# Two-layer interaction network: the leftover products of layer 1 in batches of eight tiles instead of four

## The chip, the cores and the metric

The kernel runs on one core of a Trainium2 chip. A time is that of one execution on the device in microseconds; the kernel before took 2046.02 us (median of 5 runs, 2044.9 to 2047.05). The core's engines run side by side and meet through semaphores: TensorE (PE) multiplies matrices and writes PSUM, VectorE (DVE) does elementwise and reducing work, ScalarE (ACT) evicts PSUM, GpSimd (POOL) adds tiles in layer 2, SyncE (SP) issues most of the loads. ACT issues the stores.

## The reference

A batch of 4096 rows, each with 32 fields of 16 values, goes through two layers:

```python
def _cin_layer(out, x, W, b, gamma, beta):
    r, _, e = x.shape
    h = jnp.einsum('rne,rfe->rnfe', out, x).reshape(r, -1, e)
    h = jnp.einsum('rce,oc->roe', h, W) + b[None, :, None]
    return _batchnorm(h, gamma, beta)
h1 = _cin_layer(x, x, W1, b1, g1, beta1)
out, direct1 = (h1[:, :64], h1[:, 64:])
direct2 = _cin_layer(out, x, W2, b2, g2, beta2)
agg = jnp.concatenate([direct1, direct2], axis=1)
return agg.sum(axis=-1)
```

Layer 1 multiplies every field with every field of the same row (32 x 32 products) and mixes the products into 128 channels. `_batchnorm` takes mean and variance of a channel over all rows and values, so the statistics of layer 1 must be complete before layer 2 can scale its input. Layer 2 takes the first 64 of those channels as `out`. All of it is float32.

## The kernel before, in words

A site is one value of one row: 65,536 sites in 128 tiles of T = 512. A tile's result in layer 1 is one PSUM bank: 128 channels by 512 sites.

The product of field i and field j is that of j and i, so W1 is folded beforehand and layer 1 needs about half of the products. They fall into two parts:

- The main products: for each tile, DVE writes z, four blocks of 128 products (L387, `multiply_main`), and PE multiplies them with four blocks of weights (L428), into the tile's bank. A float32 matmul is two passes on PE, so a tile has eight.
- The leftovers: 16 products of fields 16 apart. They fill only 16 rows. Eight tiles (a GROUP) share one operand `r` of 128 partitions, 32 partitions to each of four tiles; two tiles t and t+4 share the same 32. DVE multiplies the two halves of r into `zr` once for eight tiles (L373). PE multiplies 32 rows of it for each of four tiles, side by side in the array, into the banks of those four tiles (L380, `add_leftovers`). The weights for the other tile's 16 rows are zero; `w1_sb[rows, 4]` belongs to the first four tiles of the eight and `w1_sb[rows, 5]` to the last four.

The loop at L400 to L455 runs over 124 tiles. At every fourth tile it takes four banks from the pool `psum` (six buffers; `factors` has the other two banks), lets PE do the leftovers of the four tiles first (they begin the sums), then the main products of one tile after another. For tiles 0 to 3 the leftovers come after the main products of tile 1: they end the sums of tiles 0 and 1 and begin those of 2 and 3 (FIRST = 2).

`finish(t)` (L337) evicts a bank: ACT writes e (for the statistics), kept (the 64 rows that layer 2 reads; stored to DRAM as `h` after every second tile) and ed (the other 64); DVE adds e to the statistics (L115) and, after every second tile, sums ed over the embedding (L364, `sum_direct`). It is called for tile t-1 once tile t's matmuls are written. There are two buffers of e, four of z, four of the operands a and b of the main products, one each of r and zr.

The last four tiles (ENDING, L458 to L546) are done in halves of 64 channels: first the kept halves of all four, with whose statistics layer 2 can begin, then the direct halves. Their leftovers (L461, `add_leftovers_halves`) use the zr of the same group of eight as tiles 120 to 123.

The loads are on SP's queue in program order: a and b of a tile (L294, 512 KB each), `load_rem` for r (L279, 512 KB), and, spread over the loop (EARLY), the differences `xs` and the first operands of layer 2. The order of instructions on an engine is fixed when the program is built: a scheduler places them by their readiness in its own view of the program, `tc.issue_after` puts one behind another, and `queue` keeps a chain of them in order.

Of the kernel before, what the change touches and what calls it, by code (L numbers as in the profile page):

```python
# [38 lines left out]
FP = mybir.dt.float32  # L42
AF = mybir.ActivationFunctionType
ALU = mybir.AluOpType
AX = mybir.AxisListType

P = 128
# [3 lines left out]
T = 512  # L51
NC = HALF // T
NT = 2 * NC
# [4 lines left out]
GROUP = 8  # L58
# [6 lines left out]
FIRST = 2  # L65
# [5 lines left out]
def tile_cin(ctx: ExitStack, tc: tile.TileContext, xa, xb, xr, w1, w1m, w2, bn, out):  # L71
    nc = tc.nc
# [8 lines left out]
    psum = ctx.enter_context(tc.tile_pool(name="psum", bufs=6, space=bass.MemoryType.PSUM))  # L81
    factors = ctx.enter_context(tc.tile_pool(name="factors", bufs=2, space=bass.MemoryType.PSUM))
# [145 lines left out]
    def queue(engine, make):  # L228

        with tc.issue_after(lasts[engine].ins) if engine in lasts else nullcontext():  # L230
            lasts[engine] = make()
        return lasts[engine]
# [4 lines left out]
    begun = factors.tile([P, T], FP, tag="f", name="begun")  # L237
# [25 lines left out]
    with ExitStack() as one:  # L263
        lpool = one.enter_context(tc.tile_pool(name="lpool", bufs=4))
        rpool = one.enter_context(tc.tile_pool(name="rpool", bufs=1))
# [9 lines left out]
        def load_rem(g):  # L275

            r = rpool.tile([P, 2 * T], FP, tag="r", name="r")
            with tc.issue_after(loads[-1].ins) if loads else nullcontext():
                nc.sync.dma_start(r, bass.AP(xr.tensor, xr.offset + g * P * 2 * T, [[2 * T, P], [1, 2 * T]]))  # L279
            return r  # L280
# [25 lines left out]
        w1_sb = wpool.tile([P, 6, P], FP, tag="w1", name="w1_sb")  # L306
# [30 lines left out]
        pss = {}  # L337
# [4 lines left out]
        def finish(t):  # L342

            c, half = divmod(t, 2)
            ps = pss.pop(t)
            to = slice(half * KEEP, (half + 1) * KEEP)
            if half == 0:
                eds[c] = epool.tile([P, T], FP, tag="ed", name="ed")
                kept[c] = kpool.tile([KEEP, 2 * T], FP, tag="h", name="kept")
            ed = eds[c]  # L350
            e = opool.tile([P, T], FP, tag="e", name="e")
            nc.scalar.activation(e, ps, AF.Identity, bias=b1)  # L352
            stats1.add(e)
            h = kept[c]
            nc.scalar.activation(h[:, half * T : (half + 1) * T], ps[:KEEP, :], AF.Identity, bias=b1[:KEEP])
            if half == 1:
                nc.scalar.dma_start(hs[c], kept.pop(c))
            done = nc.scalar.activation(ed[to, :], ps[KEEP:, :], AF.Identity, bias=b1[KEEP:])  # L358
            if half == 1:
                sum_direct(c)  # L360
            return done

        def sum_direct(c):
            return nc.vector.tensor_reduce(  # L364
                d1[:, c * RT : (c + 1) * RT],
                eds.pop(c).rearrange("p (r e) -> p r e", e=EMB),
                AX.X,
                ALU.add,
            )

        def leftovers(r):
            zr = rpool.tile([P, T], FP, tag="zr", name="zr")
            nc.vector.tensor_tensor(zr, r[:, :T], r[:, T:], ALU.mult)  # L373
            return zr

        def add_leftovers(t, zr, begun=0):

            for k in range(4):
                rows = slice(32 * k, 32 * (k + 1))
                nc.tensor.matmul(  # L380
                    pss[t + k], w1_sb[rows, 4 + t % GROUP // 4, :], zr[rows, :], start=k >= begun, stop=k < begun
                )

        def multiply_main(z, a, b, k):

            n = k.stop - k.start
            return nc.vector.tensor_tensor(  # L387
                z[:, k],
                a.rearrange("p (a t) -> p a t", a=2)[:, k].unsqueeze(2).to_broadcast([P, n, 2, T]),
                b.rearrange("p (b t) -> p b t", b=2).unsqueeze(1).to_broadcast([P, n, 2, T]),  # L390
                ALU.mult,
            )

        def multiply_chunk(z, a, b, k, j):
            to = slice(k * T, (k + 1) * T), slice(j * T, (j + 1) * T)
            return nc.vector.tensor_tensor(z[:, k, j], a[:, to[0]], b[:, to[1]], ALU.mult)

        ending = NT - ENDING
        main = [load_main(t) for t in range(FIRST)]
        r = load_rem(0)  # L400
        for t in range(NT - ENDING):
            s = t % GROUP
            if s == 4 and t + 4 < NT:
                r = load_rem(t // GROUP + 1)
            if FIRST <= t + 1 < NT:
                main.append(load_main(t + 1))
            if s == 0 and t > 0:
                zr = leftovers(r)
            z = zpool.tile([P, 2, 2, T], FP, tag="z", name="z")
            if t < FIRST:  # L410
                for k in range(2):
                    for j in range(2):
                        product = multiply_chunk(z, *main[0], k, j)
            else:

                for k in (slice(0, 1), slice(1, 2)) if t == FIRST else (slice(0, 2),):
                    product = multiply_main(z, *main[0], k)
            main.pop(0)
            if t == FIRST - 1:
                with tc.issue_after(product.ins):  # L420
                    zr = leftovers(r)
            if s % 4 == 0:
                for k in range(4):
                    pss[t + k] = psum.tile([P, T], FP, tag="ps", name="ps")
            if s % 4 == 0 and t > 0:
                add_leftovers(t, zr)
            for m in range(4):
                nc.tensor.matmul(  # L428
                    pss[t],
                    w1_sb[:, m, :],  # L430
                    z[:, m // 2, m % 2, :],
                    start=t < FIRST and m == 0,
                    stop=t >= FIRST and m == 3,
                )
            if t == FIRST - 1:
                add_leftovers(0, zr, FIRST)
            if t > 0 and t < ending - 1:
                evicted = finish(t - 1)
            if t == 20:
                combine_weights()  # L440
                b1_swapped = const.tile([P, 1], FP, tag="b1s", name="b1_swapped")
                for x, y in ((low, high), (high, low)):
                    nc.scalar.activation(b1_swapped[x], b1[y], AF.Identity)
            if t == 0:
                continue
            with tc.issue_after(loads[-1].ins), tc.issue_after(product.ins), tc.issue_after(evicted.ins):
                if t == 12:
                    nc.vector.tensor_reduce(spread, select.rearrange("k i n f -> k (n f) i"), AX.X, ALU.max)
                if t == 14:
                    nc.vector.tensor_reduce(block, select.rearrange("k i n f -> k i (n f)"), AX.X, ALU.max)  # L450
                if t == 6:
                    nc.sync.dma_start(w2_sb, w2)
                for at, load in EARLY:
                    if t == at:
                        load()  # L455


        half_of = (low, high)  # L458

        def matmul(ps, w, z, start, stop):  # L460
            queue("pe", lambda: nc.tensor.matmul(ps, w, z, start=start, stop=stop))  # L461
# [13 lines left out]
        def add_leftovers_halves(banks, zr, direct, begun):  # L475

            for k in range(ENDING):
                rows = slice(32 * k, 32 * (k + 1))
                to = banks[k][half_of[(k + direct) % 2]]
                matmul(to, w1_sb[rows, 5, half_of[direct]], zr[rows, :], k not in begun, k in begun)  # L480

        zs = []
        for k in range(ENDING):
            if k + 1 < ENDING:
                main.append(load_main(ending + k + 1))
            zs.append(zpool.tile([P, 2, 2, T], FP, tag="z", name="z"))
            queue("dve", lambda: multiply_main(zs[k], *main.pop(0), slice(0, 2)))

        with tc.issue_after(lasts["dve"].ins):
            for t in (ending - 2, ending - 1):  # L490
                evicted = finish(t)
        banks = [psum.tile([P, T], FP, tag="ps", name="ps") for _ in range(ENDING)]
        add_leftovers_halves(banks, zr, 0, ())
        for c in range(NC - ENDING // 2, NC):
            ks = tuple(2 * c + half - ending for half in range(2))
            add_halves(banks, zs, 0, ks, True, True)
            h = kpool.tile([KEEP, 2 * T], FP, tag="h", name="kept")
            for half, k in enumerate(ks):
                at = half_of[half]
                to = h[:, half * T : (half + 1) * T]  # L500
# [28 lines left out]
        for c in range(NC - ENDING // 2, NC):  # L529
# [10 lines left out]
            for half, k in enumerate(ks):  # L540
                at = half_of[1 - half]
                bias = (b1, b1_swapped)[half][at]
                to = eds[c][half_of[half]]
# [6 lines left out]
    direct = const.tile([P, 2], FP, tag="direct", name="direct")  # L550
# [305 lines left out]
    for c in range(NC):  # L856
# [3 lines left out]
        for k, i in enumerate(STAGES):  # L860

            z = z2pool.tile([P, 4, 2, T], FP, tag="zz", name="zz")
            t = None
# [22 lines left out]
            if c > 0 or k > 0:  # L886
                t = sum_rest(z, b11, t2, (c, k) <= (1, 0), (c, k) == (NC - 1, 3))
# [121 lines left out]
```

## Time and profile before

| | |
|---|---|
| median of 5 runs | 2046.02 us (2044.9 to 2047.05) |
| profiled execution | 2045.4 us, span on the core 2043.7 us |
| layer 1 | 0 to about 490 us; layer 2 the rest |
| PE, DVE, ACT, POOL busy | 2027.5, 1959.4, 1185.4, 1487.3 us |
| leftovers in the main loop (L380) | 31 times four tiles, 248 passes |
| granted TensorE clock | 0.998 |

Layer 2, three quarters of the time, is not touched by the change. In layer 1 the matmuls of the tiles follow each other on PE; the other engines and the DMA prepare z ahead of it and clear the banks behind it. A row of the profile's groups or of its timeline has the line of the kernel, the engine, the operation and the tile that it writes and reads (out<-in). The profile counts a float32 matmul as two MATMUL instructions, one a pass.

### The profile page before, as it was taken

The page shows a single profiled execution, that of the slowest core. Times are in us where ns is not written, and L with a number is a line of the kernel's source. Part 1 is how long each engine was busy: PE and PEld are TensorE (multiplying, and loading weights), DVE is VectorE, ACT ScalarE, POOL GpSimd, SP SyncE. Part 2 cuts the span into 40 slices and gives each one's busy share as a digit, 9 for nine tenths or more (in the row PEclk, how much of TensorE's full clock was granted, in tenths as well). Part 3 has the DMA queues.
Part 4 walks back from the last instruction along what each step waited for, and adds up shares of the span by engine and source line. Part 5 has one row for each costly group of instructions (what it writes and reads, how often), then busy time and mean ns, then how long its engine had stood idle before and what let it go on. Part 6 is the DMA issues. An engine that isn't in the chain of part 4 may idle for free.

```text
span 2043.7 us, 24467 instructions
## 1 busy us (share of the span) xinstructions
PE 2027.5 (99%) x8500; PEld 888.5 (43%) x8500; DVE 1959.4 (96%) x1521; ACT 1185.4 (58%) x1914; POOL 1487.3 (73%) x525
## 2 busy tenths in 40 slices
PE   9999999999999999999999999999999999999997
PEld 3444444443344444444444444444444444444443
DVE  8998988998999999999999999999999999999998
ACT  4555555554566666655666556556656565566564
POOL 0000000002999999999999999999999999999996
PEclk9999999999999999999999999999999999999999
DMA  9999999996777777777776767777767777777661
GB/s 390 376 353 365 356 353 354 367 381 191 174 180 178 174 175 178 193 174 182 178 177 166 174 174 178 176 181 178 175 167 173 174 174 183 177 178 175 167 163 42
DMA packets 112380, 440.70 MB, mean 216 GB/s; under 512 B 13056, under 2 KB 13056, under 8 KB 103808
## 3 DMA queue, kind: packets, MB, share of 16 engines
q1 hardware_dynamic: 105840, 418.43, 73.1%
q10 hardware_dynamic: 6416, 20.72, 2.7%
q8 instruction: 66, 1.08, 0.2%
q14 instruction: 58, 0.48, 0.1%
HBM read 417.07 MB, written 22.02 MB: 215 GB/s over the span
## 4 chain that ended last, share of the span: by engine, by line
PE 98%; DVE 1%; issue 0%; POOL 0%; DMA 0%; ACT 0%; DVEq 0%; ACTq 0%; POOLq 0%
PE x L698 74%; PE ps L428 21%; PE ps L380 2%; PE ps L461 1%; DMA w1m_sb<-in_w1m 0%; POOL t L714 0%; DVE zz L667 0%; DVE d L934 0%; ACT u L659 0%; DVE both L662 0%; POOL t L703 0%; ACT both L659 0%; DVE d L833 0%; DVE t L662 0%; POOL w_sb L312 0%
## 5 line engine op out<-in xcount | busy, mean ns | idle before, releaser
L714 POOL TENSOR_TENSOR t<-zz,t 128x2048 f32<-128x2048 f32 (+1 forms) x260 | 1164.7, 4480 | 20.8 <-DVE t L662 1.0
L698 PE MATMUL x<-t,s_sb 128*64 128x512 f32 x2040 | 958.5, 592 | 0.4 <-POOL t L714 0.4
L698 PE MATMUL x<-zz,s_sb 128*64 128x512 f32 x2048 | 935.1, 593 | 0.0
L698 PE MATMUL x<-zz,w_sb 128*64 128x512 f32 x2056 | 760.7, 593 | 0.0
L703 POOL TENSOR_TENSOR t<-zz 128x512 f32<-128x512 f32 x255 | 327.1, 1283 | 515.6 <-DVE zz L667 515.2
L667 DVE TENSOR_TENSOR zz<-f,bx 128x2048 f32<-128x2048 f32 x255 | 582.7, 2285 | 19.6 <-ACT f L659 19.6
L659 ACT ACTIVATE f<-a,keep 128x512 f32<-128x512 f32 x512 | 398.2, 778 | 342.7 <-DVE zz L667 281.9
L667 DVE TENSOR_TENSOR zz<-f,b 128x2048 f32<-128x2048 f32 x255 | 583.0, 2286 | 0.1
L698 PEld LDWEIGHTS x<-t,s_sb 128*64 128x64 f32 x2040 | 279.3, 137 | 485.3 <-issue 457.0
L698 PE MATMUL x<-t,w_sb 128*64 128x512 f32 x1020 | 479.5, 593 | 0.0
L428 PE MATMUL ps<-z,w_sb 128*128 128x512 f32 x992 | 434.7, 596 | 1.7 <-POOL w_sb L312 1.6
L698 PEld LDWEIGHTS x<-zz,s_sb 128*64 128x64 f32 x2048 | 280.0, 137 | 246.4 <-issue 239.5
L387 DVE TENSOR_TENSOR z<-a,b 128x2048 f32<-128x2048 f32 (+1 forms) x127 | 288.2, 2271 | 42.6 <-PE ps L428 27.7
L428 PEld LDWEIGHTS ps<-z,w_sb 128*128 128x128 f32 x992 | 186.1, 190 | 248.9 <-issue 233.4
L698 PEld LDWEIGHTS x<-zz,w_sb 128*64 128x64 f32 x2056 | 239.7, 137 | 121.0 <-issue 119.0
L659 ACT ACTIVATE b<-zz 128x512 f32<-128x512 f32 x255 | 152.4, 598 | 187.2 <-DVE zz L667 187.2
L352 ACT ACTIVATE e<-ps,bn_sb 128x512 f32<-128x512 f32 x124 | 85.2, 687 | 218.0 <-PE ps L428 179.2
L662 DVE TENSOR_TENSOR t<-zz,b 128x512 f32<-128x512 f32 x255 | 174.0, 682 | 0.4
L698 PEld LDWEIGHTS x<-t,w_sb 128*64 128x64 f32 x1020 | 139.9, 137 | 0.0
L596 ACT ACTIVATE unread<-e,center 128x512 bf16<-128x512 f32 x122 | 86.2, 707 | 0.0
L358 ACT ACTIVATE ed<-ps,bn_sb 64x512 f32<-64x512 f32 x124 | 84.7, 683 | 2.3
L115 DVE BATCH_NORM_STATS2 stats<-e 128x6 f32<-128x512 f32 x124 | 84.9, 686 | 0.0
(103 smaller groups left out, 867.7 us busy)
## 6 DMA issues: line engine op xcount, KB each, us to landing
a<-h SPq DMA_DIRECT2D x256, 512.0 KB, 4.4
b<-in_xb SPq DMA_DIRECT2D x64, 1024.0 KB, 8.5
a<-in_xa SPq DMA_DIRECT2D x127, 512.0 KB, 7.1
b<-in_xb SPq DMA_DIRECT2D x127, 512.0 KB, 8.1
bx<-in_xb SPq DMA_DIRECT2D x64, 512.0 KB, 8.4
bx<-x SPq DMA_DIRECT2D x64, 512.0 KB, 10.1
h<-kept ACTq DMA_DIRECT2D x64, 256.0 KB, 5.7
r<-in_xr SPq DMA_DIRECT2D x16, 512.0 KB, 8.6
```

Of the source, the lines that this page charges most:

```text
L115: nc.vector.bn_stats(self.stats[:, self.at, :], h)
L352: nc.scalar.activation(e, ps, AF.Identity, bias=b1)
L358: done = nc.scalar.activation(ed[to, :], ps[KEEP:, :], AF.Identity, bias=b1[KEEP:])
L387: return nc.vector.tensor_tensor(z[:, k], a.rearrange("p (a t) -> p a t", a=2)[:, k].unsqueeze(2).to_broadcast([P, n, 2, T]), b.rearrange( ...
L428: nc.tensor.matmul(pss[t], w1_sb[:, m, :], z[:, m // 2, m % 2, :], start=t < FIRST and m == 0, stop=t >= FIRST and m == 3,)
L596: return nc.scalar.activation(unread, e[:, s], AF.Square, bias=center[:, s], accum_out=squares[:, s, c : c + 1])
L659: return queue("act", lambda: nc.scalar.activation(to, source, AF.Identity, **scale_bias))
L662: return dve(lambda: nc.vector.tensor_tensor(to, x, y, ALU.add))
L667: dve(lambda: nc.vector.tensor_tensor(z, a, b.rearrange("p (k q) t -> p k q t", k=2), ALU.mult))
L698: queue("pe", lambda: nc.tensor.matmul(self.of[x], w, b, start=start, stop=stop))
L703: queue("pool", lambda: nc.gpsimd.tensor_tensor(t2[:, 0], z[:, 1, 0], z[:, 0, 0], ALU.add))
L714: queue("pool", lambda: nc.gpsimd.tensor_tensor(t14[:, k, q], z[:, 2 + k.start : 2 + k.stop, q], twice[:, k, q], ALU.subtract))
```

## The change

The leftovers of eight tiles are done together. At every eighth tile t (8, 16, ..., 120) PE does the leftovers of tiles t-4 to t-1, which now end their sums, and those of t to t+3, which begin theirs. Tiles 4 to 7 of a group of eight begin with their main products. So up to eight banks are open at a time, and two of every eight tiles take theirs from `factors`. Nothing else is put between the two sets of four.

Eight tiles that share an r are now t-4 to t+3, so the host lays out xr in 17 groups instead of 16 (the first four and the last four tiles come twice), and the two blocks of leftover weights change places. `load_rem` is called for the next group at the second tile of each eight (for the second group at tile 3) instead of at the fifth. `finish` is called for tile t-4 instead of t-1, two tiles at a time at tiles 120 and 121. The last four tiles have a zr of their own, which DVE makes after the z of the first of them.

In the order of the built program, SP issues r ahead of the loads of tiles 4, 10, 18, 26, 34 and so on. Before, it stood ahead of tiles 5, 13, 21, 29. On DVE the next zr stands just after the statistics of the third of the four tiles that an episode of leftovers has ended.

```diff
+        def multiply_leftovers(zr, r):
+            return nc.vector.tensor_tensor(zr, r[:, :T], r[:, T:], ALU.mult)
+
         def leftovers(r):
             zr = rpool.tile([P, T], FP, tag="zr", name="zr")
-            nc.vector.tensor_tensor(zr, r[:, :T], r[:, T:], ALU.mult)
+            multiply_leftovers(zr, r)
             return zr
 
-        def add_leftovers(t, zr, begun=0):
+        def bank(t):
+            pool, tag = (psum, "ps") if t % GROUP < 6 else (factors, "f")
+            return pool.tile([P, T], FP, tag=tag, name="ps")
+
+        def ends_with_leftovers(t):
+            return t % GROUP >= 4 or t < FIRST
+
+        def add_leftovers(t, zr):
 
             for k in range(4):
                 rows = slice(32 * k, 32 * (k + 1))
-                nc.tensor.matmul(
-                    pss[t + k], w1_sb[rows, 4 + t % GROUP // 4, :], zr[rows, :], start=k >= begun, stop=k < begun
-                )
+                last = ends_with_leftovers(t + k)
+                w = w1_sb[rows, 4 + (t + 4) % GROUP // 4, :]
+                nc.tensor.matmul(pss[t + k], w, zr[rows, :], start=not last, stop=last)
...
-            if s == 4 and t + 4 < NT:
+            if s == 1 and t > 1 or t == 3:
+
                 r = load_rem(t // GROUP + 1)
...
             if s % 4 == 0:
                 for k in range(4):
-                    pss[t + k] = psum.tile([P, T], FP, tag="ps", name="ps")
-            if s % 4 == 0 and t > 0:
+                    pss[t + k] = bank(t + k)
+            if s == 0 and t > 0:
+                add_leftovers(t - 4, zr)
                 add_leftovers(t, zr)
             for m in range(4):
                 nc.tensor.matmul(
                     pss[t],
                     w1_sb[:, m, :],
                     z[:, m // 2, m % 2, :],
-                    start=t < FIRST and m == 0,
-                    stop=t >= FIRST and m == 3,
+                    start=ends_with_leftovers(t) and m == 0,
+                    stop=not ends_with_leftovers(t) and m == 3,
                 )
             if t == FIRST - 1:
-                add_leftovers(0, zr, FIRST)
-            if t > 0 and t < ending - 1:
-                evicted = finish(t - 1)
+                add_leftovers(0, zr)
+
+            if t >= ending - 2:
+                evicted = finish(t - 2)
+            elif t >= ending - 4:
+                for done in range(2 * t - ending, 2 * t - ending + 2):
+                    evicted = finish(done)
+            elif t >= 4:
+                evicted = finish(t - 4)
...
-            if t == 0:
+            if t < 4:
                 continue
...
-                matmul(to, w1_sb[rows, 5, half_of[direct]], zr[rows, :], k not in begun, k in begun)
+                matmul(to, w1_sb[rows, 4, half_of[direct]], zr[rows, :], k not in begun, k in begun)
...
             queue("dve", lambda: multiply_main(zs[k], *main.pop(0), slice(0, 2)))
+            if k == 0:
+                zr = rpool.tile([P, T], FP, tag="zr", name="zr")
+                queue("dve", lambda: multiply_leftovers(zr, r))
...
-    xr = np.stack([xt[:, :16], xt[:, 16:]], axis=2).reshape(NT // GROUP, GROUP // 4, 4, 16, 2, T)
-    xr = xr.transpose(0, 2, 1, 3, 4, 5).reshape(NT // GROUP, P, 2, T)
+
+    xr = np.stack([xt[:, :16], xt[:, 16:]], axis=2)
+    xr = np.concatenate([xr[:4], xr, xr[-4:]]).reshape(NT // GROUP + 1, GROUP // 4, 4, 16, 2, T)
+    xr = xr.transpose(0, 2, 1, 3, 4, 5).reshape(NT // GROUP + 1, P, 2, T)
```

## The prediction

> **What bounds the kernel now.** I read the page first: busy times, then the chain that ended last.
>
> ```profile
> PE 2027.5 (99%) x8500; PEld 888.5 (43%) x8500; DVE 1959.4 (96%) x1521; ACT 1185.4 (58%) x1914; POOL 1487.3 (73%) x525
> PE 98%; DVE 1%; issue 0%; POOL 0%; DMA 0%; ACT 0%; DVEq 0%; ACTq 0%; POOLq 0%
> ```
>
> TensorE (PE) is the bound in both layers; layer 1 is the first 490 us of 2043.7. What shortens PE's own work there shortens the kernel, as long as VectorE (DVE) and the DMA keep ahead. Next the timeline of PE in a settled stretch (start, length, engine, line):
>
> ```profile
> 99.39 1.14 PE L380 MATMUL ps<-zr,w_sb 32*128 32x512 f32 x8
> 100.46 14.00 PE L428 MATMUL ps<-z,w_sb 128*128 128x512 f32 x32
> 114.39 1.14 PE L380 MATMUL ps<-zr,w_sb 32*128 32x512 f32 x8
> ```
>
> Every four tiles take 15.00 us, to the hundredth: 32 instructions of the main products and eight of leftovers (four tiles side by side, two passes each). No stall. The same timeline cut so narrowly that single passes show, PE's weight loads (PEld) with it:
>
> ```profile
> 98.87 0.59 PE L428 MATMUL ps<-z,w_sb 128*128 128x512 f32 x1
> 99.39 0.31 PEld L380 LDWEIGHTS ps<-zr,w_sb 32*128 32x128 f32 x8 [0.76 <-issue]
> 99.39 0.71 PE L380 MATMUL ps<-zr,w_sb 32*128 32x512 f32 x4
> 99.92 0.61 PE L380 MATMUL ps<-zr,w_sb 32*128 32x512 f32 x4
> 100.46 0.70 PE L428 MATMUL ps<-z,w_sb 128*128 128x512 f32 x1
> 100.99 1.02 PE L428 MATMUL ps<-z,w_sb 128*128 128x512 f32 x2
> ```
>
> In the main stream a pass starts 0.43 us after the one before. Around the leftovers the four steps are 0.52, 0.53, 0.54 and 0.53. The first pass after each change of shape lasts 0.70 to 0.71 instead of 0.59 to 0.61, so it really begins 0.10 us into its row: the true steps are 0.62 (into the leftovers), 0.43 (between their two passes), 0.64 (back) and 0.43. So it is the two changes of shape that cost, about 0.2 us each, and not the passes between. Per episode: 15.00 - 34 x 0.4294 = 0.40 us.
>
> Last, who waits in DVE from 40 to 474 us, and the start of the run, where the cover is thinnest:
>
> ```profile
> DVE z L387 <- PE ps L428: 26.6, 39, 2.3
> DVE z L387 <- DMA b<-in_xb: 14.0, 11, 3.2
> ...
> 21.23 2.27 DVE L387 TENSOR_TENSOR z<-a,b 128x2048 f32<-128x2048 f32 x1
> 23.42 0.68 DVE L364 TENSOR_REDUCE d<-ed 128x32 f32<-128x512 f32 x1
> 24.38 1.14 PE L380 MATMUL ps<-zr,w_sb 32*128 32x512 f32 x8
> ...
> 17.41 0.69 ACT L352 ACTIVATE e<-ps,bn_sb 128x512 f32<-128x512 f32 x1 [8.40 <-PE ps L380]
> 19.39 0.69 ACT L352 ACTIVATE e<-ps,bn_sb 128x512 f32<-128x512 f32 x1
> ```
>
> DVE mostly waits for PE to free a z: it is four tiles ahead, a lead of 9 us (the z that ends at 121.49 is used at 130.46). ScalarE (ACT) evicts one tile every 1.98 us when it need not wait, beginning 1.16 us after the leftovers start (16.25).
>
> **The change, part by part.**
>
> *PE.* The main loop has the same 124 leftover matmuls, in 16 episodes instead of 31. If passes 2 to 3 follow like 1 to 2 (0.43), each of the 15 merges removes one pair of shape changes: 15 x 0.40 = **-6.0 us**. Bounds: nothing saved, if each four cost their 0.40 wherever they stand; no row offers more than 6.0. I take 6.0, since the step between passes 1 and 2 is the nearest row.
>
> [...] The row above shows eight loads, the second four for the same row groups, begun within 0.31 us while the first passes run for 0.71. [...]
>
> *The settled loop.* Let T be the start of a merged episode: PE starts tile 0 of the eight at T + 1.07 + 2 x 0.43 = T+1.93, then one tile per 3.435. DVE's order in the changed kernel at T is: z of tile 3, stats of the old tiles 4 and 5, a reduce, stats 6, zr, stats 7, a reduce, z of tile 4. The old tiles 4 to 7 are all finished only by this episode, so these wait for ACT: its last eviction ends at T + 1.16 + 3 x 1.98 + 1.94 = T+9.04, the reduce (0.60 to the next) is over at 9.64, z of tile 4 ends at T+11.9. PE wants it at T + 1.93 + 4 x 3.435 = T+15.7. So the lead falls from 9.0 to 3.8 us at that tile but holds: cost 0. An aggregate (0.69 + 0.15) or a negation on ACT (0.63) takes at most 0.9 of it. DVE's work is unchanged but for one zr. PSUM: tile 4's bank is empty at T+3.1, reused at T+15.7. On ACT the evictions, with the stores of h on its queue, move three tiles later (h of tile 0 is first read near tile 92), and the stores of xd with them. POOL has nothing here.
>
> *SP's queue.* r now stands ahead of the loads of tiles 4, 10, 18, 26 and so on, and there are 17 of them. Its own data are wanted about 21 us later, so r is covered. It also changes places with layer 2's early loads near tiles 76 to 117; all of those are wanted only at 487 us. What is queued behind r comes 512 KB later, about 1.2 us at the 419 GB/s of the saturated stretch from 15 to 55 us. The longest DVE waits for DMA lie between 320 and 360 us, where the lead fell from 9.07 to 3.64, a loss of 5.4. On the leanest tile 5.4 - 3.8 = 1.6 would show; on the other seven not. Bounds 0 and 3.2 (the longest wait); I take 1.6 / 8 = **+0.2**.
>
> *The start.* The second r is now issued ahead of tile 4's loads and waits for the first zr to end (14.63). Before, tile 4's two loads landed at 18.9 and 20.3 and this r at 21.5; exchanged, r lands near 19 and the operands by 21.5. DVE has zr and the reduce ahead of z of tile 4 now: it starts at 21.23 + 2 x 0.60 = 22.43 (loads just covered) and ends at 24.70. PE, without the episode at 24.38, wants it at 24.29: a wait of 24.77 - 24.29 = **+0.5**; bounds 0 (DVE's extra 1.2 against its cover of 1.95, if PE came no earlier) and 1.7 (tile 4's data 1.2 later). For tiles 10 to 20 the same count, carried on, leaves z 0.1 to 1 us early; I take 0 and leave the rest to the range.
>
> *The end.* The last four tiles' zr is made after z of the first of them, and behind the burst of evictions of tiles 116 to 119. With T for the episode at tile 120, the tail begins at E = T + 1.93 + 4 x 3.435 + 0.09 = T+15.8. DVE: stats 119 ends at T+8.4, aggregate and reduce by 9.8, then four z of 2.19 net, two stats, zr and a reduce of 0.60 each: the last z ends at T + 9.8 + 11.2 = T+21.0 = E+5.3. It was E+2.4 before (474.54 + 2.29 against E = 474.43). PE wants it after the tail's leftovers and 16 half-width passes, E + 1.02 + 3.44 = E+4.5: **+0.9**, and all that follows (keep factors, layer 2's first factor) waits with it. Bounds 0 and 2.5 (another 1.6 of late loads).
>
> Sum: -6.0 + 0.2 + 0.5 + 0.9 = -4.4 us. The profiled execution took 2045.4, 0.6 below the median of 2046.0; on the median this is **2041.6 us**.
>
> **Rivals.**
> *Covers spent.* The gain comes but start and tail take their upper bounds (1.7 + 2.5) and a dense DMA stretch another 1.6: -0.2, 2045.8. For it: leads of under 1 us at the start and DVE busy all the time from 20 to 55 us. Against: the DMA has nothing idle in that stretch, so later issues do not make later landings.
> [...]
> *A new wait in every group.* DVE at T hangs on ACT, and ACT on DVE (two e buffers; the waits show ACT held by DVE's stats for 17.3 us, 11 times). If the z of tile 4 comes x us later than PE wants it, that is 15 x. From x = 0.6, that is 4.4 us beyond my time for it, the kernel is slower by over 0.2%; x = 1 gives 2056.6. Against: the 3.8 us, from rows that vary by hundredths.
>
> **How the numbers follow.** 0.2% is 4.1 us, about what a measurement of this kernel can tell from no change, and my forecast lies just past it. Forecast 0.62 (2039.6 to 2043; of this 0.50 under 2041.9), covers spent 0.16, no gain of switching 0.09, a wait per group 0.13. So faster 0.50, same 0.37, slower 0.13. The range 2039.6 (6.0 saved, nothing lost, 0.4 of scatter) to 2047.0 leaves out most of the last rival and little else.
>
> **What the profile after would show.** Right: leftovers as x16, 2.0 us, 29.6 us apart; first passes of 0.70 once per eight tiles; a wait of some 0.5 us for z near 24 and some 0.9 in the tail. Wrong: steps over 0.5 inside the x16; PE waiting for DVE at the fifth tile of each eight; DVE waiting for r.

## The result, and the profile after

The changed kernel took 2050.06 us (median of 23 executions, 2042.89 to 2053.05), the kernel before 2045.96 on the same chip (41 executions, 2044.83 to 2047.78). The ratio of the means is 1.0018, 95% interval 1.0012 to 1.0023: slower by 0.18%, where the prediction had 0.2% faster. The spread is as telling as the median: 10.2 us against 3.0. Its fastest execution, 2042.89, is still 1.3 us above the 2041.6 that was predicted.

The profiled execution took 2046.01 us (span 2044.3), one of the faster ones; a second profile of the same kernel, in the experiments, caught one of 2050.32. The page of the first, busy times and chain:

```profile
PE 2023.0 (99%) x8500; PEld 893.5 (44%) x8500; DVE 1959.0 (96%) x1522; ACT 1185.3 (58%) x1914; POOL 1486.9 (73%) x525
PE 92%; DMA 3%; DVE 2%; ACT 1%; issue 1%; POOL 0%; SPq 0%; DVEq 0%; ACTq 0%; POOLq 0%
```

PE is busy 4.5 us less than before, and the chain now passes through DMA and DVE for 5% of the span, where PE alone had 98%. The work became less and a wait took its place. First the work, in PE's timeline (start, length):

```profile
98.39 2.00 PE L393 MATMUL ps<-zr,w_sb 32*128 32x512 f32 x16
100.31 27.73 PE L441 MATMUL ps<-z,w_sb 128*128 128x512 f32 x64
127.98 2.00 PE L393 MATMUL ps<-zr,w_sb 32*128 32x512 f32 x16
129.91 0.70 PE L441 MATMUL ps<-z,w_sb 128*128 128x512 f32 x1
```

Eight tiles take 127.98 - 98.39 = 29.59 us, where twice four took 30.00. That is 0.41 per merged pair, as forecast. Then what PE waits for from 10 to 490 us (total, times, longest), where before it waited for nothing from 20 us on:

```profile
PE ps L441 <- ACT e L353: 3.1, 1, 3.1
PE ps L441 <- DVE z L398: 1.5, 2, 1.2
PE ps L441 <- ACT ed L359: 0.7, 1, 0.7
```

DVE's waits from 40 to 474 us, which answer to those of before:

```profile
DVE z L398 <- DMA b<-in_xb: 21.7, 18, 3.6
DVE stats L116 <- ACT e L353: 11.4, 16, 1.3
...
DVE z L398 <- PE ps L441: 3.5, 3, 3.1
```

Before, DVE mostly waited for PE to free a z (26.6 us), a sign of being ahead; now that is 3.5 (and 1.1 for a z that the leftovers' passes held up), and it waits for loads and for ACT.

The steps between PE's passes give the places and the sizes: 0.45 us beyond the usual 0.43 ahead of tile 4, 0.90 ahead of tile 20, 1.33 ahead of tile 90 and 3.25 ahead of tile 92, in all 5.9. The place of the two largest, in the timelines of the same kernel: DVE, then ACT, then PE.

```profile
332.89 2.29 DVE L398 TENSOR_TENSOR z<-a,b 128x2048 f32<-128x2048 f32 x1 [2.66 <-DMA b<-in_xb]
337.08 2.29 DVE L398 TENSOR_TENSOR z<-a,b 128x2048 f32<-128x2048 f32 x1 [1.90 <-DMA b<-in_xb]
343.01 2.29 DVE L398 TENSOR_TENSOR z<-a,b 128x2048 f32<-128x2048 f32 x1 [3.63 <-DMA b<-in_xb]
345.58 2.29 DVE L398 TENSOR_TENSOR z<-a,b 128x2048 f32<-128x2048 f32 x1 [0.28 <-DMA b<-in_xb]
347.79 1.28 DVE L116 BATCH_NORM_STATS2 stats<-e 128x6 f32<-128x512 f32 x2
...
352.54 0.69 DVE L365 TENSOR_REDUCE d<-ed 128x32 f32<-128x512 f32 x1 [0.58 <-ACT ed L359]
353.15 2.28 DVE L398 TENSOR_TENSOR z<-a,b 128x2048 f32<-128x2048 f32 x1
...
348.57 0.69 ACT L353 ACTIVATE e<-ps,bn_sb 128x512 f32<-128x512 f32 x1 [8.34 <-DVE stats L116]
...
345.36 7.13 PE L441 MATMUL ps<-z,w_sb 128*128 128x512 f32 x16 [1.16 <-DVE z L398]
355.57 8.82 PE L441 MATMUL ps<-z,w_sb 128*128 128x512 f32 x20 [3.08 <-ACT e L353]
```

It is read from the top. The operands b of four z in a row land late, 8.5 us in sum (the last z is tile 91's). The statistics of tiles 84 and 85 stand behind that z in DVE's order, so they run at 347.79. Until then both e buffers are full and ACT stands still for 8.34 us. Only now can the evictions of the episode go on, one every 1.97 to 2.29 us, and the z of tile 92, the fifth of its eight, stands behind the statistics of all four. It begins at 353.15 and PE stands still until 355.57. PE's wait is put down to ACT, but what came late first is a load.

The loads on SP's queue that do not belong to a tile, there and in the kernel before (the timeline of SP, cut to these rows):

```profile
320.73 0.56 SPq L191 DMA_DIRECT2D xs<-in_xb  x1
327.24 0.59 SPq L191 DMA_DIRECT2D xs<-in_xb  x1
329.12 0.33 SPq L280 DMA_DIRECT2D r<-in_xr  x1
340.39 0.54 SPq L168 DMA_DIRECT2D a<-h  x1
```

```profile
317.77 0.56 SPq L190 DMA_DIRECT2D xs<-in_xb  x1
321.95 0.89 SPq L190 DMA_DIRECT2D xs<-in_xb  x1
336.68 0.59 SPq L167 DMA_DIRECT2D a<-h  x1
339.52 0.34 SPq L279 DMA_DIRECT2D r<-in_xr  x1
```

r has moved from behind the heap into it, right behind the second xs, 512 KB each. Before, the lead of z fell there too, to 3.64, and PE felt nothing. The xs loads come every 24 tiles, at tiles 14 and 16, 38 and 40, 62 and 64, 86 and 88. The leads of z in the first profile of the changed kernel show the same grid: 0.15, 0.24, 0.28 and 0.15 us at the fifth tiles 20, 44, 68 and 92, that is six tiles after the first xs of each pair, and 0.97 to 3.78 at the other fifth tiles from 12 on. PE waited at tiles 20 and 92 of these, not at 44 and 68.

The tail is as forecast: from the start of the last main pass of the loop to layer 2's first matmul 17.85 us, where it was 16.91 (+0.94).

### The profile page after: what moved, and what is told of

Read it like the earlier page. It is cut to its first block, busy times and chain, and to the rows that moved or that the text cites. A ratio compares the mean times of both kernels' runs of the same rounds, so it can differ in the third digit from the quotient of the medians.

```text
span 2044.3 us, 24488 instructions
## 1 busy us (share of the span) xinstructions
PE 2023.0 (99%) x8500; PEld 893.5 (44%) x8500; DVE 1959.0 (96%) x1522; ACT 1185.3 (58%) x1914; POOL 1486.9 (73%) x525
## 4 chain that ended last, share of the span: by engine, by line
PE 92%; DMA 3%; DVE 2%; ACT 1%; issue 1%; POOL 0%; SPq 0%; DVEq 0%; ACTq 0%; POOLq 0%
PE x L720 74%; PE ps L441 16%; DMA b<-in_xb 2%; DMA a<-in_xa 1%; PE ps L393 1%; DVE z L398 1%; PE ps L480 1%; ACT e L353 0%; ACT ed L359 0%; ACT kept L356 0%; DVE stats L116 0%; DMA w1m_sb<-in_w1m 0%; POOL t L736 0%; DVE zz L689 0%; SPq L295 0%
## 5 line engine op out<-in xcount | busy, mean ns | idle before, releaser
L398 DVE TENSOR_TENSOR z<-a,b 128x2048 f32<-128x2048 f32 (+1 forms) x127 | 286.7, 2265 | 27.3 <-DMA b<-in_xb 22.5
L116 DVE BATCH_NORM_STATS2 stats<-e 128x6 f32<-128x512 f32 x124 | 83.8, 686 | 11.4 <-ACT e L353 11.4
```

Source lines behind the costliest of these rows:

```text
L116: nc.vector.bn_stats(self.stats[:, self.at, :], h)
L398: return nc.vector.tensor_tensor(z[:, k], a.rearrange("p (a t) -> p a t", a=2)[:, k].unsqueeze(2).to_broadcast([P, n, 2, T]), b.rearrange( ...
```

## Experiments

Three theories were written down before the first runs. Supply: the lead of z at the fifth tile of each eight is now under 4 us and no longer covers loads that land late, so it is the loads that cost. Chain: the four evictions that an episode ends, with DVE and ACT taking turns, delay the fifth z by themselves. The moved r: its place on SP's queue alone makes the operands late. All times below are medians; each batch of kernels has its own runs of the kernel before.

| kernel | median us (range) | ratio to before (95%) |
|---|---|---|
| changed, again | 2049.48 (2043.19 to 2052.30) | 1.0015 (1.0006 to 1.0023) |
| changed, no xs loads | 2041.14 (2039.95 to 2042.61) | 0.9976 (0.9966 to 0.9985) |
| changed, r at the fifth tile | 2046.27 (2041.12 to 2049.46) | 1.0001 (0.9992 to 1.0011) |
| changed, statistics behind z | 2041.76 (2040.29 to 2047.25) | 0.9982 (0.9974 to 0.9991) |
| changed, three e | 2048.13 (2041.02 to 2052.05) | 1.0004 (0.9995 to 1.0014) |
| statistics behind z, r at the fifth tile | 2042.90 (2041.00 to 2047.70) | 0.9988 (0.9979 to 0.9997) |
| before, no xs loads | 2045.38 (2044.92 to 2048.12) | 0.9999 (0.9990 to 1.0007) |
| changed, no xs loads, six waits put in | 2091.89 (2091.77 to 2094.05) | 1.0225 (1.0212 to 1.0238) |
| statistics behind z, three e | 2043.51 (2040.41 to 2047.53) | 0.9988 (0.9979 to 0.9997) |
| statistics behind z, xs two tiles earlier | 2041.34 (2040.32 to 2046.98) | 0.9981 (0.9973 to 0.9990) |
| before, three z | 2046.25 (2045.08 to 2048.81) | 1.0004 (0.9995 to 1.0013) |
| changed, xs two tiles earlier | 2044.46 (2042.08 to 2046.74) | 0.9993 (0.9984 to 1.0002) |

### The changed kernel again

No edit.

> The changed kernel as it is, for the profile of another execution. Three theories of where the 6.0 us that PE saves go. Supply: DVE's lead over PE has fallen to 0 to 4 us at the fifth tile of each eight, and in the stretches with the xs loads, r and layer 2's first operands the DMA lands later than that lead, by amounts that differ from one execution to the next; PE then waits at tiles 18 to 20, 42 to 44, 66 to 68 and 90 to 92 and nowhere else, in different sizes, 3 to 12 us in all; median 2049 to 2051. Chain: the evictions and statistics of the four tiles that an episode ends hold the next z back in every group of eight; PE waits by about the same amount in most of the 15 groups. The moved r: DVE waits for r (before zr) or for the loads right behind it, in most groups.

2049.48 us, the same picture. Its profiled execution, 2050.32, is near the median and shows what the first profile could not. What PE waits for:

```profile
PE ps L441 <- DVE z L398: 5.1, 3, 4.0
PE ps L441 <- ACT ed L359: 1.3, 1, 1.3
```

Windows of the same execution around the wait of 3.95 us ahead of 357.31 (columns: busy us and instructions of PE, PEld, DVE, ACT, POOL; granted clock; DMA share; GB/s):

```profile
357.00:358.00 1.00, 0.69 (x1) 0.50 (x2) 1.00 (x3) 0.97 (x2) 0.00 (x0) 0.50 0.20 82
358.00:359.00 1.00, 1.00 (x2) 0.34 (x1) 1.00 (x1) 0.97 (x3) 0.00 (x0) 0.50 0.72 156
361.00:362.00 1.00, 1.00 (x3) 0.48 (x2) 1.00 (x2) 0.97 (x3) 0.00 (x0) 0.50 1.06 397
362.00:363.00 1.00, 1.00 (x3) 0.28 (x3) 1.00 (x1) 0.62 (x1) 0.00 (x0) 0.76 1.00 410
363.00:364.00 1.00, 1.00 (x4) 0.52 (x3) 1.00 (x3) 0.00 (x0) 0.00 (x0) 1.00 1.08 418
```

The clock was halved until about 362.5: passes 0.85 us apart, some 2.6 us lost behind the wait. In the first profile the wait of 3.08 us left the clock at 1.00. The steps of this execution: 0.44 ahead of tile 4, 1.51 ahead of 20, 1.2 ahead of 90 and 91, 4.11 ahead of 92 and the rest slow passes behind it: 9.9 in all. It is 4.3 us slower than the first profiled execution, and the stalls differ by 4.0.

### Without the xs loads

```diff
-        EARLY += [(at + 2 * k, lambda g=g, k=k: load_x(g, k)) for k in range(2)]
...
         xd = xpool.tile([P, 2 * T], FP, tag="xd", name="xd")
+        nc.gpsimd.memset(xs, 1.0)
```

> The changed kernel without the eight xs loads (4 MB in all): the buffer is filled with ones once, and the negations, differences and stores go on, so that the differences that layer 2 uses are wrong and everything else is as before. Supply: the waits at tiles 18 to 20, 42, 66 and 90 go, what stays is 0.5 at tile 4 and 0.9 in the tail; 2041 to 2043, executions within 1.5 us of each other. Chain: no change, 2049 to 2051. The moved r: r still stands ahead of loads, 2047 to 2050.

2041.14 us, with a range of 2.7. PE waits for nothing from 20 us on, and the lead at the fifth tile is 3.1 to 3.8 us from tile 28 to the end, as the prediction had worked out from the rows of before. DVE's waits from 18 to 480 us, where the changed kernel waited 21.7 us, 18 times, for b:

```profile
DVE stats L116 <- ACT e L353: 16.4, 19, 1.3
DVE d L365 <- ACT ed L359: 10.5, 19, 0.6
DVE z L398 <- DMA b<-in_xb: 7.3, 10, 1.5
```

The evictions and their order are untouched here, and DVE waits more for ACT than in the changed kernel (there 11.4), yet nothing reaches PE. As a cost in every eight the chain is refuted. The eight loads of 512 KB are what takes the gain away, some 8.5 us.

### r at the fifth tile, as before the change

```diff
-            if s == 1 and t > 1 or t == 3:
+            if s == 4 or t == 121:
```

> The changed kernel with r loaded at the fifth tile of each eight, as before the change (and the last r at tile 121). Supply: r no longer follows the second xs directly, 1.2 us less ahead of tiles 18, 42, 66 and 90, but it is again next to layer 2's loads near 92; a part of the loss goes, 2045 to 2049; tile 4's wait of 0.5 goes too. Chain: 2049 to 2051 less 0.5. The moved r: nearly all goes, 2041.5 to 2043.5.

2046.27 us, but three executions of eleven at 2041 to 2042 and the others up to 2049.5. The profiled one is of the good kind: no wait of PE, yet a lead of 0.38 us at tile 92. r's place is worth some 3 us in the median (the interval overlaps a little with that of the changed kernel, so the size is uncertain) and does not cure the spread.

### The statistics of two tiles behind the z of the fifth

```diff
         def finish(t, later=None):
...
-            stats1.add(e)
+            if later is None:
+                stats1.add(e)
+            else:
+                later.append(lambda: stats1.add(e))
...
+                if s == 4:
+                    with tc.issue_after(product.ins):
+                        while deferred:
+                            deferred.pop(0)()
-                evicted = finish(t - 4)
+                evicted = finish(t - 4, deferred if s in (2, 3) and t > 8 else None)
```

(the sum over ed of the later tile is deferred in the same way).

> The changed kernel with the statistics and the reduce of the third and fourth tile that an episode ends put behind the z of the fifth tile of the eight on DVE (ACT and the loads keep their order). z of the fifth tile then ends at about T+8.6 instead of T+11.9 and its load for the tile four on is issued as much sooner: lead 7 us instead of 3.8. Supply: the lead covers most of the late landings, 2042 to 2046. Chain: 2041.5 to 2043, no wait in any group. The moved r: 2048 to 2050.

2041.76 us: 0.18% faster than before. The settled lead is 7.15 us. The loads are as late as ever; what PE waits for, and the late operands on DVE:

```profile
PE ps L448 <- ACT ed L364: 1.8, 3, 0.9
PE ps L448 <- DVE z L405: 0.3, 1, 0.3
```

```profile
DVE z L405 <- DMA b<-in_xb: 20.5, 17, 4.3
```

DVE still waits 20.5 us for b, and PE 2.1 instead of the 5.3 of the changed kernel's first profile. The same lateness costs less where the lead is larger.

### Three buffers of e

```diff
-        opool = one.enter_context(tc.tile_pool(name="opool", bufs=2))
+        opool = one.enter_context(tc.tile_pool(name="opool", bufs=3))
```

> The changed kernel with three buffers for the evicted tile e instead of two. In the changed kernel's profile ScalarE stood still for 8.34 us before 348.57 because both e buffers waited for statistics that stood in VectorE's order behind a z whose operands were late; the four evictions that the episode ends then ran one after the other, and the z of the fifth tile came 3.25 us late. Supply x chain (the late load is made worse by the chain behind it): one eviction more can go ahead, worth one ScalarE turn of 1.98 us in that episode; the wait of 3 to 4 us at tile 92 falls to 1 to 2, and since it then stays shorter than the 3.95 us after which TensorE ran at half clock in the repeat (another 2.6 us), the median falls from 2049.5 to 2045-2047.5. Supply alone (the z is late because its own operands are): 2049 to 2050, no change. The settled lead at the fifth tile stays 3.8 in both.

2048.13 us, between the two expectations and with a range of 11 us. ACT's wait for statistics fell from 37.7 to 6.4 us, so that link of the chain is gone, but the lead at tile 92 was 0.15 even in an execution of 2041.37. A gain over the changed kernel isn't shown (the intervals overlap).

### Both repairs together

```diff
 (the statistics as above, and)
-            if s == 1 and t > 1 or t == 3:
+            if s == 4 or t == 121:
```

> Both repairs together: statistics of the third and fourth tile behind the z of the fifth (lead 7.15 where settled), and the leftovers' load r issued at the fifth tile of each eight again, as before the change. Supply: the two lost different things, so it is below either alone (2041.8 and 2046.3): 2040 to 2041.5, with no wait of TensorE beyond 20 us but one of under 0.5 near 92, and a spread of under 3 us. If r's place only ever mattered through the small lead, nothing is left for it to give: 2041.5 to 2042.

2042.90 us: neither expectation; no better than the deferred statistics alone. DVE's waits from 40 to 480 us show why the old place of r does not suit the merged episodes:

```profile
DVE zr L380 <- DMA r<-in_xr: 16.0, 7, 3.1
DVE z L405 <- DMA b<-in_xb: 10.9, 8, 2.2
```

r itself is late now, seven times. The waits for b that it saves return as waits for r.

### The kernel before without the xs loads

The same edit as in the changed kernel.

> The kernel before, without the xs loads (xs is set once, so layer 2's differences are wrong, as in the run of the changed kernel without them). Supply: the kernel before has a lead of 9 us at every tile, and no TensorE wait in its settled stretch; the loads cost it nothing, so taking them away gives 2046.0 within 0.5, against the 8.3 us that it gave the changed kernel. If the loads cost something by themselves (memory traffic, the queue, layer 2's start) beside the lead: 2043 or less.

2045.38 us, ratio 0.9999 (0.9990 to 1.0007). The loads cost the kernel before nothing that these runs can tell; its lead stays at 8.97 at every fifth tile from 28 on. The same loads cost the changed kernel 8.5 us. So the loads cost something only together with what the change brought: the smaller lead, r's new place and the four evictions in a row. Which of the three it is, this pair of runs does not tell.

### Waits put into the version without the xs loads

```diff
+        held = w1_sb[:, :4].rearrange("p k o -> p (k o)")
+        STALLS = {30: (512,), 46: (512, 512), 62: (512, 512, 128), 78: (512,) * 3, 102: (512, 512, 512, 128), 110: (512,) * 4}
...
+            for n in STALLS.get(t, ()):
+                nc.gpsimd.tensor_tensor(held[:, :n], held[:, :n], ones[:, :n], ALU.mult)
```

> The changed kernel without xs loads (no TensorE wait beyond 20 us, 2041.1), with six waits put into layer 1: ahead of the main products of tiles 30, 46, 62, 78, 102 and 110 GpSimd multiplies a part of the weights by one in place, in one to four steps of 512 columns, with 128 more in two of them. By the 1.28 us that such a step of 512 took GpSimd in layer 2 and 0.45 for one of 128, with some 0.4 of signalling, TensorE should stand still for 1.7, 3.0, 3.4, 4.2, 4.7 and 5.5 us, 22.5 in all. If a wait costs only its own length: 2063.6, every pass after it 0.43 us apart, granted clock 1.00 throughout. If TensorE's clock is halved after a wait of about 4 us, as the repeat of the changed kernel showed once (3.95 us of wait, then half clock until 362.5, 2.6 us lost): the three or four longest cost some 2.6 more each, 2071 to 2075, with the granted clock at 0.50 behind them and at 1.00 behind the short ones. [...]

2091.89 us; the expected total was missed by 17 us and more. The waits came to 31.2 us instead of 22.5, since GpSimd's steps took up to 4.98 us instead of 1.28; the 0.4 of signalling was an estimate, and from the end of GpSimd's last step to PE's next pass the profile has 0.05 us at all six. The rest of the miss was not traced. No wait fell between 0.4 and 5.4. What the waits do is clear all the same. PE's timeline at the first and at two long ones, and the windows behind three (columns as above):

```profile
122.70 7.13 PE L448 MATMUL ps<-z,w_sb 128*128 128x512 f32 x16 [0.41 <-POOL w_sb L446]
188.67 9.54 PE L448 MATMUL ps<-z,w_sb 128*128 128x512 f32 x16 [5.46 <-POOL w_sb L446]
327.19 8.56 PE L448 MATMUL ps<-z,w_sb 128*128 128x512 f32 x16 [6.95 <-POOL w_sb L446]
```

```profile
122.00:126.00 4.00, 3.58 (x9) 1.62 (x9) 4.00 (x3) 1.94 (x3) 0.65 (x1) 1.00 1.03 421
188.70:192.70 4.00, 4.00 (x5) 1.80 (x6) 0.00 (x0) 0.00 (x0) 0.00 (x0) 0.50 1.00 401
327.20:331.20 4.00, 4.00 (x6) 1.82 (x7) 0.59 (x2) 0.00 (x0) 0.00 (x0) 0.64 0.99 342
```

The same 16 passes take 7.13 us after the short wait, 9.54 and 8.56 after long ones. All five waits of 5.5 to 7.0 us were followed by a halved clock (0.64 in the third window is a mean over its end); tile by tile against the version without them, the slow passes cost 2.5, 2.1, 1.5, 1.5 and 2.6 us. The version without the waits has a clock of 1.00 in every window from 60 to 460 us. So the slow stretch behind a long wait is here a consequence of the wait, not of the loads.

### Three e with the deferred statistics, and xs moved

```diff
 (the statistics as above, and)
-        opool = one.enter_context(tc.tile_pool(name="opool", bufs=2))
+        opool = one.enter_context(tc.tile_pool(name="opool", bufs=3))
```

> The statistics behind the z of the fifth tile, and three buffers for e. In the run with two, ScalarE still waited 30.9 us in all for VectorE's statistics (up to 7.0); with three buffers alone that fell to 6.4 but the time hardly moved (2048.1). Supply (what is missing is lead over late loads, and ScalarE's turns are not it): 2041.3 to 2042.2, as with two. Chain (what is left of the waits, 2.8 us in that profile at tiles 21, 92 and 93, comes from evictions held by the deferred statistics): 2039.5 to 2040.5, and no wait for ed at tiles 92 and 93.

2043.51 us, and the fastest execution no faster than with two e. It is not the gain that the chain predicts; against two e no difference is shown.

```diff
 (the statistics as above, and)
-        at = 14 + 24 * g
+        at = 12 + 24 * g
```

> The statistics behind the z of the fifth tile, and the xs loads, with what uses them, two tiles earlier (at 12, 14, 36, 38 and so on in place of 14, 16, 38, 40), further ahead of r, which stands at 17, 25, 33. Supply, if it is the heap of xs, r and layer 2's early loads within six tiles that makes them late: the waits left near tile 92 shrink, 2040.5 to 2041.5, with a spread under 3 us. Supply, if it is the sum of all loads (the DMA shares of this layer are 0.95 to 1.03 everywhere): no change, 2041.5 to 2042.5, or worse by a us, since the xs of the first group then fall into the start, where leads are under 1 us.

2041.34 us, the fastest of the complete versions: nine of eleven executions lie at 2040.3 to 2042.5, and in the profiled one PE waits for nothing in layer 1 beyond 20 us, with a lead of 2.4 at tile 92 where it was 0.15 (at tile 93 it is 0.29). The heap's version is favoured; the difference from 2041.76 is within the scatter.

### The kernel before with three z

```diff
-        zpool = one.enter_context(tc.tile_pool(name="zpool", bufs=4))
+        zpool = one.enter_context(tc.tile_pool(name="zpool", bufs=3))
+        zlast = one.enter_context(tc.tile_pool(name="zlast", bufs=1))
...
-            zs.append(zpool.tile([P, 2, 2, T], FP, tag="z", name="z"))
+            zs.append((zlast if k == 3 else zpool).tile([P, 2, 2, T], FP, tag="z", name="z"))
```

> The kernel before with three z buffers in its main loop instead of four (the fourth is kept for the tail's last tile). Nothing else is changed: leftovers in fours, one eviction per tile, r at the fifth tile. Its settled lead falls by one tile of 3.75 us, from 9.0 to some 5.2, about as far as the repaired version's and more than the changed kernel's 3.8. Supply: a lead of 5.2 is about spent where the profile of before lost 5.4 (tiles 92 to 95) and at the start, where it had 2.5 to 4.4 with four: waits of 1 to 3 us there, 2047 to 2050, with a spread of more than 3 us, with no chain of four evictions anywhere. If the chain of evictions is what loses the time and the lead alone does not: 2046.0 within 0.5.

2046.25 us: no cost in the median, against supply's 2047 to 2050. The profiled execution, 2048.81 and the slowest of the eleven, shows the mechanism beginning: the settled lead is 5.54 at the fifth tile and 4.4 at the last tile of every four, it falls to 0.05 at tiles 90 and 93, and PE waits there once:

```profile
PE ps L429 <- DVE z L388: 1.0, 1, 1.0
```

So with leads of 4.4 to 5.5 these loads reached PE once in that execution, for 1.0 us. By itself a loss of 3.5 us of lead cannot explain 8.5 us; the changed kernel goes 1.7 lower at the fifth tile, has r in the heap, and has ACT and DVE waiting for each other behind the late z.

### xs two tiles earlier, alone

```diff
-        at = 14 + 24 * g
+        at = 12 + 24 * g
```

> The changed kernel with the xs loads and what uses them two tiles earlier (12, 14, 36, 38 and so on in place of 14, 16, 38, 40), and nothing else: the lead of 3.8 us at the fifth tile stays. With the statistics deferred this move changed 2041.8 to 2041.3. Supply, heap: r of the changed kernel stands at 17, 41, 65 and 89, one tile behind the second xs load, so that 2 MB are issued ahead of four tiles' operands; apart, the worst loss falls and with it the time, to 2043 to 2047. Supply, sum: the small lead loses as much to the same bytes two tiles earlier, 2049 to 2050.5. In both the spread stays over 5 us, since leads of under 1 us are left at tiles 12 to 20.

(xs is two loads of 512 KB, so with r it is 1.5 MB, not the 2 that I wrote.) 2044.46 us, ratio 0.9993 (0.9984 to 1.0002), where the unchanged order has 1.0018: more than half of the loss goes by taking xs and r apart, with the same bytes, the same lead of 3.8 and the same chain. DVE waits 13.0 us for b instead of 21.7, and the longest such wait is 2.1 instead of 3.6. PE waits 1.8 us in two waits, the longer 0.9. So more than half of the loss is the heap within a few tiles; the sum of the loads is the same and cannot explain that part.

## Why the prediction was wrong

**The merges, -6.0: right.** 29.59 us for eight tiles, 0.41 saved by each of 15 merges, and PE's busy time is down, from 2027.5 to 2023.0 us. Inside the x16 the passes start at 98.92, 99.35 and 99.78, 0.43 us apart, across the seam between the two sets of four too. Of the sixteen weight loads eight are made at the start, as before (98.38, 0.31 us in all), four come at 98.92 (0.20), while the second pass runs, and four at 99.35 (0.21), while the third does.

**The settled loop, lead 3.8: right in size, wrong in use.** Without the xs loads the lead is the 3.8 that was counted. "But holds: cost 0" was judged against DVE's and ACT's own rows; the lead has one more use, to cover loads.

**SP's queue, +0.2: the step that failed.** It was the term that should have held the loss, and it was mis-sized in three ways. First, "1.6 / 8": dividing by eight took the worst place to be a random tile. 24 tiles are three times eight, so the xs loads keep their phase to the episodes: six tiles after the first xs of each pair stands a fifth tile (20, 44, 68, 92), in every execution. Nor were "the other seven" safe: tile 90, the third of its eight, made PE wait 1.3 and 1.0 us in the two profiles, though its z is 7.4 us ahead when the xs loads are left out. Second, the loss of lead was taken from the kernel before, 5.4, with only r added. In the changed kernel the late z also holds up the statistics behind it, those hold ACT (8.34 us), and the evictions then run in turns: PE lost 4.6 us at tiles 90 and 92 in the first profile and 5.3 in the second, above the upper bound of 3.2. Third, a wait of 3.95 us cost more than its length: the clock was halved after it, another 2.6. In the profile near the median these make up 4.11 + 1.2 + 2.6 us against the 0.2. No row in the profile of the kernel before showed a halved clock behind a wait; PE's longest wait there is 1.6 us, at the start.

**The start, +0.5: right at tile 4 (0.45), but not in every execution, and "for tiles 10 to 20 I take 0" was wrong.** The four profiles with r's new place and a full clock at the start (both of the changed kernel, statistics behind z, three e) have this wait, 0.44 to 0.47. Five others with r at the same place (both without the xs loads, statistics behind z with three e, and the two with xs earlier) have a granted clock of 0.50 from about 9 to 12 us instead; there PE comes to tile 4 later and does not wait, but tile 8 begins at 41.1 to 41.7 us instead of 40.1 to 40.5. Ahead of tile 20 the two profiles of the changed kernel lost 0.9 and 1.5 us. The count had left z there 0.1 to 1 us early, which is no cover; it is also the first place of the xs loads, and the two causes were not parted.

**The tail, +0.9: right** (0.94).

With the stalls of the second profile beyond the forecast's terms, 9.9 - 0.5 - 0.2, the forecast of 2041.6 becomes 2050.8, and that execution took 2050.3. Without the loads that cause them the kernel takes 2041.1.

Of the rivals, "covers spent" named the cause, late loads in a dense stretch, and priced it too low: it allowed that stretch 1.6. Its other terms, the upper bounds of start and tail (1.7 and 2.5), did not come: 0.45 at tile 4 and 0.94 in the tail. "A new wait in every group" was wrong as a wait per group. "No gain of switching" (0.09) was wrong: each merge saved 0.41 us. Against "covers spent" stood "later issues do not make later landings" in a saturated stretch; moving the xs loads by two tiles changed the ratio by 0.0025, some 5 us, so here the order of issue does count.

What stays open: how the loss divides between r's new place, the smaller lead and the chain of ACT and DVE. Each of three edits recovers a part (some 3, 5 and 8 us), and they do not add. No kernel was run that has a lead of 3.8 and one eviction at a time; the nearest, the kernel before with three z, has 4.4 at its thinnest tiles and lost nothing in the median. Open too is why in the first profile the DMA, busy all through the stretch (a share of 0.94 to 1.12 in every slice), moved 217 to 310 GB/s in some slices of 1.3 us between 310 and 362 us and up to 429 in others; the version without the xs loads has such slices as well (225 to 280).

## What to carry to other kernels

A lead is a stock that several costs draw on. When a change spends part of it, look up every place where the stock ran low before, ask whether that place always meets the thinnest tile, and count what is queued behind the late instruction too. And take the spread of the executions from the stock that is left: here a change that did save its 6 us was slower in the median because it waited for loads whose lateness differs from one execution to the next. Deferring work that nobody waits for, behind the operand that PE waits for, gave the gain back.

## What the runs showed of the hardware

- Beyond the start of layer 1 PE's granted clock fell to 0.50 after waits of 3.95 us and of 5.5 to 7.0 us (six of six) and stayed at 1.00 after one of 3.08; no wait lay between 3.08 and 3.95. The half clock then cost 1.5 to 2.6 us; behind the wait of 3.95 it lasted 5.2 (357.31 to about 362.5).
- At the start the half clock came behind shorter waits. The wait of PE for GpSimd's first weights, ahead of its first main pass, lasted 1.4 to 1.6 us in five profiles, and the clock stayed at 1.00; it lasted 1.9 to 2.7 us in the other nine, variants of the kernel before among them, and in all nine the clock was at 0.50 for some 3 us just behind it, between 8 and 14 us.
- The same order of loads gave different executions. The changed program with leads under 1 us spread over 10.2 us (2042.89 to 2053.05), the one with its xs loads left out over 2.7 (2039.95 to 2042.61).
- In the run with the waits put in, GpSimd's in-place multiplication of 128x512 took 1.26 us in eight of fifteen cases and 3.19 to 4.98 in the other seven. All eight began while no z multiplication ran on DVE, all seven while one did. A z that began on DVE during a step was longer as well: 3.03 us instead of 2.28 at 121.76.
